# A macaron block: the written order of the first feed-forward's first two tiles

## The chip, the core and the metric

One core of one Trainium2 chip runs the whole kernel. The metric is the device time of one execution in microseconds (us), the median of several runs. The engines are TensorE (PE, with its weight loads PEld), VectorE (DVE), ScalarE (ACT), GpSimd (POOL) and SyncE (SP, which here only issues transfers). Each works through its own queue in order; they wait for each other by semaphores.

## What is computed

2048 tokens with 1024 features, all in float32, pass a feed-forward, an attention over a convolution, and the same feed-forward again:

```
x = x + 0.5 * ffn(layernorm(x))
x = x + attn(layernorm(x))
x = x + 0.5 * ffn(layernorm(x))

def ffn(x):                                   # weight 1024x1024, 8 experts
    routing   = softmax(x @ gate_w.T)
    in_scale  = routing @ in_channel_scale
    out_scale = routing @ out_channel_scale
    return (x * in_scale) @ sign(weight).T * out_scale + bias
```

The change is in the first feed-forward alone, in how its first tiles are put in order.

## The kernel before, in words

The first feed-forward works on 16 tiles of 128 tokens. A tile goes through these stages, each a method of `Ffn`:

- `norm`: mean and variance by DVE (`normalize`, L155 to L161), the inverse root by POOL as a power (L162), and the normalized row `xn` by ACT with a shift from POOL (L169, L170) or by DVE alone (L166).
- `add_bias` (L192): a transfer issued by POOL adds the halved bias `hbias` onto the token row in SBUF, for the residual.
- `transpose` (L200, L201): eight 128x128 transposes by PE in two banks of PSUM, copied to `xnT`.
- `gate` (L208, L216): PE multiplies with the gate weights, ACT copies the result `lgs`.
- `route` (L221 to L232): PE folds the logits (`lg`), DVE takes the maximum (L223), ACT the exp (L226), DVE the reciprocal and the routing in a high and a low part (`rhl`).
- `turn` (L239, L241): PE transposes the routing (`rt`), DVE copies it (`rT`).
- `scale` (L251 to L265): PE multiplies `rT` with a table of channel scales, `tables` (`is`, eight matmuls); for each half of 512 features DVE multiplies `xnT` with it, a high part `y` is rounded (L264, ACT), and POOL subtracts for the low part (L265).
- `out_scale` (L274, L276): PE makes the output scale (`po`), ACT halves it into `os`.
- `main` (L287 to L297): for each half of 512 outputs 16 matmuls of 128x512, high and low part of eight chunks against the signs of the weights, `sw`; DVE multiplies with `os` and adds to the token row.

Two tiles' chains run ahead of the main products. The loop `run` puts the stages of the tiles t+1 to t+4 around the two halves of tile t. After a tile's main product come the second norm and its transposes for the attention part (`norm_x2`, `transpose_x2`, L408 to L419).

The loop's instructions are ordered by a scheduler, while those of `begin`, L621 to L690, stand under `tc.manual_schedule()`: each engine gets them in the order of the program text. `begin` loads the gate weights and a bias row by ACT's queue, two token rows, six of the eight weight chunks and a third token row by SP's, and four pieces of the tables by POOL's. It builds `tables` from them (L664, `table_terms`: L142, L143), normalizes and transposes tiles 0 and 1, spreads the bias over 128 partitions by matmuls with a column of halves (`hb`, L659) that DVE copies (L660), and then goes tile 0 and tile 1 through gate, route, turn and scale. The signs of the weight chunks (L633, ACT) stand in between. Tile 0's main product takes both halves together, with tile 2's transposes and tile 3's norm between its chunks 5 and 6; the loop starts with tile 1.

Two sets of banks matter: `tr` (two banks) holds transposes and input scales in turn, `mm` (two) the main products. A small bias for the attention part each (`conv_b` to `bo`, L699) is loaded by POOL behind `begin`.

Of the kernel before, what the change touches and what calls it, by code (L numbers as in the profile page):

```python
# [24 lines left out]
def kernel(  # L25
# [87 lines left out]
    halves = const.tile([1, P], F32, name="halves")  # L113
    nc.gpsimd.memset(halves, 0.5)
# [13 lines left out]
    def table_loads(tmp):  # L128

        raw = tmp[:, 0, 0:NB]  # L130
        for n, src in enumerate((ics, ocs)):
            for h in range(NH2):
                nc.gpsimd.dma_start(
                    out=raw[ts(2 * n + h, QC), :],
                    in_=src[:, ts(h, NB)].unsqueeze(0).broadcast_to([4, E, NB]),
                )
        return raw

    def table_terms(raw, upper):


        nc.vector.tensor_scalar(raw, raw, lower, None, ALU.mult)  # L142
        nc.vector.scalar_tensor_tensor(tables, upper.bitcast(F32), sides, raw, ALU.mult, ALU.add)  # L143
# [7 lines left out]
    def normalize(dst, src, name, pinned=False, on_vector=False):  # L151

        stats = small.tile([P, NH2, 6], F32, name=f"st_{name}", tag="stats")
        for h in range(NH2):
            ins = nc.vector.bn_stats(out=stats[:, h, :], in_=src[:, ts(h, NB)])  # L155
            if pinned:
                pin(ins)
        mv = small.tile([P, 2], F32, name=f"mv_{name}", tag="mv")
        nc.vector.bn_aggr(out=mv, in_=stats)
        rstd = small.tile([P, 1], F32, name=f"rs_{name}", tag="rstd")  # L160
        nc.vector.tensor_scalar(rstd, mv[:, 1:2], EPS, None, ALU.add)  # L161
        nc.gpsimd.tensor_tensor(rstd, rstd, nhalf, ALU.pow)  # L162
        if on_vector:
            for h in range(on_vector):
                cols = ts(h, D // on_vector)
                nc.vector.tensor_scalar(dst[:, cols], src[:, cols], mv[:, 0:1], rstd, ALU.subtract, ALU.mult)  # L166
            return
        shift = small.tile([P, 1], F32, name=f"sh_{name}", tag="shift")
        nc.gpsimd.tensor_scalar(shift, mv[:, 0:1], rstd, -1.0, ALU.mult, ALU.mult)  # L169
        nc.scalar.activation(dst, src, AF.Identity, bias=shift, scale=rstd)  # L170

    class Ffn:
# [6 lines left out]
        def __init__(self, name, sw, work, xnp, first, end, row, ahead, after, between, beside, kept=1, leave=None):  # L179
            self.kept, self.leave = kept, leave or (lambda t, h: None)  # L180
            self.name, self.sw, self.work, self.xnp, self.first, self.end = name, sw, work, xnp, first, end
            self.row, self.ahead, self.after, self.between, self.beside = row, ahead, after, between, beside
            self.xns, self.xnTs, self.lgps, self.routs, self.rTs, self.oscs, self.ys = ({} for _ in range(7))

        def norm(self, t, pinned=False, on_vector=False):
            for n in range(t, min(t + 2, self.end)):
                self.ahead(n)
            self.xns[t] = self.xnp.tile([P, D], F32, name=f"xn_{self.name}_{t}", tag="xn")
            normalize(self.xns[t], self.row(t), f"{self.name}_{t}", pinned, on_vector)
# [4 lines left out]
        def transpose(self, t, copy=nc.scalar.copy):  # L194
            xn = self.xns.pop(t)
            xnT = self.work.tile([P, DC, P], F32, name=f"xnT_{self.name}_{t}", tag="xnT", bufs=3)
            for h in range(DC // 4):
                tr = bank("tr", [P, 4, P], f"tr_{self.name}_{t}_{h}")
                for c in range(4):
                    nc.tensor.transpose(tr[:, c, :], xn[:, ts(4 * h + c, P)], ident)  # L200
                copy(xnT[:, 4 * h : 4 * h + 4, :], tr)  # L201
            self.xnTs[t] = xnT
# [16 lines left out]
        def route(self, t):  # L219
# [6 lines left out]
            nc.scalar.activation(rout, lg, AF.Exp, bias=nmax, accum_out=rsum)  # L226
            nc.vector.reciprocal(rsum, rsum)
# [16 lines left out]
        def scale(self, t, copy=nc.scalar.copy, out=False):  # L244
# [15 lines left out]
            for h, sc in enumerate(scs):  # L260
                y = xnT[:, 4 * h : 4 * h + 4, :]
                nc.vector.tensor_tensor(y, y, sc, ALU.mult)
                yh, yl = (yhl[:, n, 4 * h : 4 * h + 4, :] for n in range(2))
                copy(yh, y)  # L264
                nc.gpsimd.tensor_tensor(yl, y, yh.bitcast(F32), ALU.subtract)  # L265
# [13 lines left out]
        def main(self, t, *halves, between=None, at=DC - 2):  # L279
            y, osc, xrow = self.ys[t], self.oscs[t], self.row(t)  # L280
            pms = {h: bank("mm", [P, NB], f"pm_{self.name}_{t}_{h}") for h in halves}
            for c in range(DC):
                if between and c == at:
                    between()
                for h, pm in pms.items():
                    for n in range(2):
                        nc.tensor.matmul(  # L287
                            pm,
                            lhsT=y[:, n, c, :],
                            rhs=self.sw[:, c, ts(h, NB)],  # L290
                            start=(c == 0 and n == 0),
                            stop=(c == DC - 1 and n == 1),
                        )
            for h, pm in pms.items():
                o, xt = osc[:, ts(h, NB)], xrow[:, ts(h, NB)]
                nc.vector.tensor_tensor(pm, pm, o, ALU.mult)  # L296
                nc.vector.tensor_tensor(xt, xt, pm, ALU.add)  # L297
                self.leave(t, h)
            if NH2 - 1 in pms:
                del self.ys[t], self.oscs[t]  # L300
# [19 lines left out]
        def run(self):  # L320
# [3 lines left out]
            for t in range(self.first, self.end):  # L324
                self.on(self.gate, t + 2)
                if t + 1 in self.ys:
                    self.out_scale(t + 1)
                elif t + 1 < self.end:
                    self.scale(t + 1, out=True)
                route, turn = (lambda stage=stage: self.on(stage, t + 2) for stage in (self.route, self.turn))  # L330
                begun = t not in self.ys
                if begun:
                    route()
                else:
                    self.main(t, 0, between=route, at=DC // 2)
# [4 lines left out]
                if begun:  # L340
                    turn()
                else:
                    self.main(t, 1, between=turn, at=DC // 2)
# [46 lines left out]
    def norm_x2(t):  # L390
        xn = x2ns[t] = xnp.tile([P, D], F32, name=f"x2n_{t}", tag="xn")
# [3 lines left out]
        normalize(xn, x1.pop(t), f"x2_{t}", on_vector=2 * (t + 1 == NT))  # L395
# [225 lines left out]
    def begin(ffn, work):  # L621
# [5 lines left out]
        def load_raw(c):  # L627
            raws[c] = cwp.tile([P, D], F32, name=f"raw_{c}", tag="cw")
# [6 lines left out]
        tmp = work.tile([P, 2, D], F32, name="tables_raw", tag="y")  # L635
        upper = work.tile([P, 2, D], F32R, name="tables_upper", tag="y")[:, 0, 0:NB]

        rows = work.tile([P, D], F32, name="gate_rows", tag="osc")[0:DC, :]
        brow = work.tile([P, D], F32, name="bias_row", tag="osc")[0:1, :]
        nc.scalar.dma_start(out=rows, in_=gate_t.rearrange("(c p) e -> c (p e)", p=P))  # L640
        nc.scalar.dma_start(out=brow, in_=bias)
        load_x(0)
        load_x(1)
        for c in range(6):
            load_raw(c)
        load_x(2)
        raw = table_loads(tmp)
# [5 lines left out]
        ffn.norm(0)  # L653
        ffn.norm(1, on_vector=True)
        ffn.transpose(0)
        ffn.transpose(1, nc.vector.tensor_copy)
        for h in range(NH2):
            hb = bank("acc", [P, NB], f"hb_{h}")
            nc.tensor.matmul(hb, lhsT=halves, rhs=brow[:, ts(h, NB)], start=True, stop=True)  # L659
            nc.vector.tensor_copy(hbias[:, ts(h, NB)], hb)  # L660
        ffn.add_bias(0)
        ffn.add_bias(1)
        ffn.gate(0)
        nc.scalar.copy(upper, raw)  # L664
        ffn.route(0)
        table_terms(raw, upper)
        ffn.gate(1)
        sign(0)
        load_raw(6)
        ffn.turn(0)  # L670
        ffn.route(1)
        sign(1)
        load_raw(7)
        load_x(3)
        ffn.scale(0)
        ffn.turn(1)
        sign(2, 3)
        ffn.scale(1, nc.vector.tensor_copy)
        sign(4, 5)
        ffn.norm(2, on_vector=True)  # L680
        ffn.add_bias(2)
        sign(6)
        ffn.out_scale(0)
        sign(7)

        def third():
            ffn.transpose(2, nc.vector.tensor_copy)
            ffn.norm(3, on_vector=True)
            ffn.add_bias(3)

        ffn.main(0, 0, 1, between=third)

    with ExitStack() as ph:
# [4 lines left out]
        for dst, src in ((conv_b_sb, conv_b), (bq_sb, bq), (bk_sb, bk), (bv_sb, bv), (bo_sb, bo)):  # L698
            tc.keep_in_program_order(nc.gpsimd.dma_start(out=dst, in_=src))  # L699
        ffn.run()  # L700
# [275 lines left out]
    ffn.run()  # L976
# [55 lines left out]
```

## Time and profile before

| what | value |
|---|---|
| runs | 976.38, 977.24, 980.49 us; median 977.24 |
| the profiled execution | 980.25 us; its span in the trace 978.0 us |
| granted TensorE clock, mean | 0.999 |
| DVE, ACT, POOL busy | 67%, 42%, 26% of the span |
| tile 3's first main matmul to tile 4's, tile 4's to tile 5's | 10.81, 10.84 us |
| HBM read, written | 81.18 MB, 37.85 MB |
| signs of the weights on ACT, one of 128x1024 | 1.05 us |
| low part on POOL, one of 128x512 | 1.28 us |
| add on DVE, one of 128x512 | 0.69 us |

In the profile's lines of instructions in order of time, the columns are the start and the length in us of a merged group, the engine, the line of the kernel, the operation, output <- inputs, sizes and the number of instructions; in brackets stands how long the engine sat idle before it, and what released it. In the lines of waits they are the waiting engine and line, what it waited for, and the total, the count and the longest in us. A timeline's name has no tile number, so tiles are told apart by their order.

### The profile page before, as it was taken

To read this page: it belongs to the slowest core of one execution; us is meant where nothing else is said; L and a number is where in the kernel's file an instruction comes from. 1 tells how busy PE (TensorE), PEld (TensorE's weight loads), DVE (VectorE), ACT (ScalarE), POOL (GpSimd) and SP (SyncE) were. 2 spreads that over 40 slices of the span, in tenths; PEclk is the share of its full clock that TensorE was granted. 3 is DMA by queue.
4 is the path that set the end of the run, shared out by engine and by line. 5 is a ranking of instruction groups with operands and counts; after the bars stand their busy time and mean duration, and the time that the engine had idled before them with its cause. 6 is when DMAs were issued, how large, how long until landed. Compare 5 with 4: busy or idle time off the path is not lost.

```text
span 978.0 us, 13872 instructions
## 1 busy us (share of the span) xinstructions
PE 955.0 (98%) x5068; PEld 624.4 (64%) x5068; DVE 652.0 (67%) x1229; ACT 409.4 (42%) x1117; POOL 256.1 (26%) x327
## 2 busy tenths in 40 slices
PE   5999999999999999999999999999999999999998
PEld 3778888776666666655555455545554556778776
DVE  4879887789976556636656455645565655777764
ACT  3576675331111111125546244526461663444440
POOL 3654553320011011003303121212122312444341
PEclk9999999999999999999999999999999999999999
DMA  8866653598496775335030430044003226646331
GB/s 251 235 164 193 183 174 131 196 274 332 155 276 183 183 183 122 93 108 226 15 116 1 152 113 17 1 151 151 1 1 139 62 39 210 173 135 174 108 108 65
DMA packets 36820, 136.69 MB, mean 140 GB/s; under 512 B 4297, under 2 KB 5321, under 8 KB 34834
## 3 DMA queue, kind: packets, MB, share of 16 engines
q1 hardware_dynamic: 27472, 98.15, 27.9%
q0 software_dynamic: 8544, 29.64, 15.9%
q10 hardware_dynamic: 738, 8.02, 2.2%
q8 instruction: 40, 0.66, 0.3%
q14 instruction: 26, 0.21, 0.1%
HBM read 81.18 MB, written 37.85 MB: 122 GB/s over the span
## 4 chain that ended last, share of the span: by engine, by line
PE 45%; issue 26%; POOL 5%; DVE 1%; DMA 0%; ACT 0%; POOLq 0%; DVEq 0%
PE cv L521 22%; PE pm_f L287 13%; POOL xr L807 3%; PE pp L941 2%; POOL p L863 2%; PE acc L922 2%; PE tr_f L200 1%; PE pq L830 1%; PE lgp_f L208 1%; PE is_f L251 1%; PE ao L905 1%; PE pt L892 1%; PE sc L851 0%; DMA qkv<-y 0%; DVE y L618 0%
## 5 line engine op out<-in xcount | busy, mean ns | idle before, releaser
L287 PE MATMUL pm_f<-sw,y_f 128*128 128x512 f32 x1024 | 263.6, 405 | 0.2 <-DVE x L297 0.2
L287 PEld LDWEIGHTS pm_f<-sw,y_f 128*128 128x128 f32 x1024 | 184.7, 189 | 40.6 <-DVE x L297 0.4
L521 PE MATMUL cv<-v,u 128*128 128x342 f32 x576 | 166.0, 450 | 0.0
L521 PEld LDWEIGHTS cv<-v,u 128*128 128x128 f32 x576 | 109.0, 189 | 56.8
L863 POOL TENSOR_SCALAR_AFFINE_SELECT p<-p 128x512 f32<-128x512 f32 x64 | 39.9, 647 | 282.1 <-ACT p L861 282.1
L876 ACT ACTIVATE p<-p,anm 128x128 f32<-128x128 f32 x256 | 99.0, 389 | 16.8 <-DVE anm L873 16.8
L265 POOL TENSOR_TENSOR y_f<-xnT_f,y_f 128x512 fp32r<-128x512 f32 x64 | 81.1, 1281 | 59.8 <-ACT y_f L264 59.0
L538 ACT ACTIVATE m<-cv 128x342 f32<-128x342 f32 x42 | 19.2, 457 | 159.0 <-PE cv L521 154.8
L861 ACT COPY p<-sc 128x512 f32<-128x512 f32 x64 | 34.3, 589 | 111.4 <-PE sc L851 111.3
L873 DVE TENSOR_REDUCE anm<-p 128x4 f32<-128x512 f32 x64 | 40.9, 681 | 49.1 <-POOL p L863 49.1
L296 DVE TENSOR_TENSOR pm_f<-pm_f,os_f 128x512 f32<-128x512 f32 x64 | 44.4, 694 | 35.4 <-PE pm_f L287 35.1
L922 PE MATMUL acc<-oT,wo_sb 128*128 128x512 f32 x128 | 67.2, 616 | 0.4 <-DVE oT L914 0.4
L830 PE MATMUL pq<-qkv,wq_sb 128*128 128x512 f32 x128 | 61.0, 596 | 0.0
L830 PE MATMUL pq<-qkv,wk_sb 128*128 128x512 f32 x128 | 60.1, 592 | 0.0
L521 PE MATMUL cv<-v,g 128*128 128x342 f32 (+2 forms) x224 | 57.1, 415 | 0.9 <-DVE v L443 0.9
L941 PE MATMUL pp<-pw_sb,o2T 128*128 128x512 f32 x128 | 57.4, 599 | 0.4
L814 PE MATMUL pv<-wv_sb,qkv 128*128 128x512 f32 x128 | 56.1, 592 | 0.0
L509 DVE SCALAR_TENSOR_TENSOR u<-g,u 128x1024 f32<-128x1024 f32 x18 | 22.0, 1222 | 43.7 <-issue 30.1
L521 PEld LDWEIGHTS cv<-v,g 128*128 128x128 f32 x224 | 39.7, 190 | 17.6 <-DVE v L443 1.3
L201 ACT COPY xnT_f<-tr_f 128x512 f32<-128x512 f32 x60 | 32.6, 590 | 42.0 <-PE tr_f L200 42.0
L876 ACT ACTIVATION_READ_ACCUMULATOR p<-p,anm 128x1 f32 x256 | 48.0, 188 | 0.0
L884 DVE TENSOR_TENSOR p<-p,asum 128x512 f32<-128x512 f32 x64 | 45.6, 712 | 2.4 <-DVE asum L883 0.3
(146 smaller groups left out, 1485.5 us busy)
## 6 DMA issues: line engine op xcount, KB each, us to landing
g<-in_conv_w_dram SPq DMA_DIRECT2D x28, 512.0 KB, 4.8
u<-in_conv_w_dram POOLq DMA_DIRECT2D x24, 512.0 KB, 6.3
x<-in_x_dram SPq DMA_DIRECT2D x16, 512.0 KB, 5.1
raw<-in_weight_t_dram SPq DMA_DIRECT2D x16, 512.0 KB, 7.0
x<-hbias POOLq DMA_DIRECT2D x16, 512.0 KB, 5.6
x<-x SPq DMA_DIRECT2D x16, 512.0 KB, 5.3
xr<-x SPq DMA_DIRECT2D x16, 512.0 KB, 7.1
x<-xr SPq DMA_DIRECT2D x16, 512.0 KB, 4.0
```

Of the source, the lines that this page charges most:

```text
L265: nc.gpsimd.tensor_tensor(yl, y, yh.bitcast(F32), ALU.subtract)
L287: nc.tensor.matmul(pm, lhsT=y[:, n, c, :], rhs=self.sw[:, c, ts(h, NB)], start=(c == 0 and n == 0), stop=(c == DC - 1 and n == 1),)
L296: nc.vector.tensor_tensor(pm, pm, o, ALU.mult)
L521: nc.tensor.matmul(accs[w, k][:, lo:hi], lhsT=uk[:, c, :], rhs=V[k][:, c, lo:hi], start=(c == 0), stop=(c == DC - 1),)
L814: nc.tensor.matmul(pv, lhsT=qkvs[g][2][:, c, ts(b, P)], rhs=wv_sb[:, c, ts(half, NB)], start=(c == 0), stop=(c == WC - 1),)
L830: nc.tensor.matmul(pq, lhsT=w_sb[:, c, ts(hp, P)], rhs=qkvs[g][n][:, c, :], start=(c == 0), stop=(c == WC - 1),)
L863: nc.gpsimd.affine_select(out=p, in_=p, pattern=[[0, BPG], [-1, P]], compare_op=ALU.is_ge, fill=NEG_INF, base=0, channel_multiplier=1,)
L873: nc.vector.tensor_reduce(nmax, p, AX.X, ALU.max, negate=True)
L876: nc.scalar.activation(p[:, b, :], p[:, b, :], AF.Exp, bias=nmax[:, b : b + 1], accum_out=asum[:, b : b + 1],)
L884: nc.vector.tensor_tensor(p, p, asum.unsqueeze(2).broadcast_to([P, BPG, P]), ALU.mult)
L922: nc.tensor.matmul(accs[g][m], lhsT=wo_sb[:, hp, ts(m, P)], rhs=oT, start=(hp == 0), stop=(hp == NHP - 1),)
L941: nc.tensor.matmul(pp, lhsT=o2T[:, m, ts(b, P)], rhs=pw_sb[:, m, ts(h, NB)], start=(m == 0), stop=(m == WC - 1),)
```

## The change

`begin` is written anew and goes further, to the end of tile 1's main product; the loop starts with tile 2.

- Loads: all eight weight chunks, the bias (spread over 128 partitions by the transfer itself), and token rows 2 to 5 are issued by SP at once. Weight chunks 6 and 7 lie in buffers of the token rows. The five small biases for the attention part go to SP's queue.
- The bias is halved by ACT in place. The column of halves, the four instructions of `hb` and their copies are gone.
- Norm is split into its sums and its application; tiles 0 to 3 are applied by DVE, tile 0 in two halves.
- Tile 0 goes through gate and route ahead of tile 1's transposes. The tables are made in two parts of 64 rows, the input scales' first, with DVE's product placed between the exp and the reciprocal.
- The low part of tile 0's first half is made by DVE.
- The stages of tiles 1 to 4 and signs 3 to 7 are put between the chunks of the main products of tiles 0 and 1. Tile 0's last two chunks are done for one half and then the other, and each half's end on DVE follows its last chunk.

```diff
+    def upper_terms(raw, upper, n):
+        nc.scalar.copy(upper[ts(n, P // 2), :], raw[ts(n, P // 2), :])
+
+    def lower_terms(raw, n):
+        at = ts(n, P // 2)
+        nc.vector.tensor_scalar(raw[at, :], raw[at, :], lower[at, :], None, ALU.mult)
...
-        def main(self, t, *halves, between=None, at=DC - 2):
...
+        def main(self, t, *halves, beside={}, apart=DC):
...
+            for c, h in [(c, h) for c in range(apart) for h in halves] + [
+                (c, h) for h in halves for c in range(apart, DC)
+            ]:
+                if h == halves[0] and c in beside:
+                    beside[c]()
...
+                if c == DC - 1:
+                    o, xt = self.oscs[t][:, ts(h, NB)], xrow[:, ts(h, NB)]
+                    nc.vector.tensor_tensor(pms[h], pms[h], o, ALU.mult)
+                    nc.vector.tensor_tensor(xt, xt, pms[h], ALU.add)
...
-        for h in range(NH2):
-            hb = bank("acc", [P, NB], f"hb_{h}")
-            nc.tensor.matmul(hb, lhsT=halves, rhs=brow[:, ts(h, NB)], start=True, stop=True)
-            nc.vector.tensor_copy(hbias[:, ts(h, NB)], hb)
...
+        for c in range(DC):
             load_raw(c)
+            if c == 5:
+                load_x(2)
+        nc.sync.dma_start(out=hbias, in_=bias.broadcast_to([P, D]))
+        load_x(3)
+        load_x(4)
+        load_x(5)
+        table_loads(raw)
...
+        on_vector = (nc.vector.tensor_copy,) * 2
+        ffn.norm_sums(0, on_vector=2)()
+        norm = ffn.norm_sums(1, on_vector=1)
+        ffn.transpose(0)
+        norm()
+        ffn.gate(0)
+        upper_terms(raw, upper, 0)
+        ffn.route(0, lambda: lower_terms(raw, 0))
+        table_terms(raw, upper, 0)
+        ffn.transpose(1)
+        ffn.turn(0)
+        sign(0, 1)
+        ffn.scale(0, lows=(nc.vector, nc.gpsimd))
+        upper_terms(raw, upper, 1)
+        lower_terms(raw, 1)
+        table_terms(raw, upper, 1)
+        ffn.gate(1)
+        sign(2)
...
+        def halve():
+            nc.scalar.mul(hbias, hbias, 0.5)
+
+        def sums(t, on_vector=False):
+            norms[t] = ffn.norm_sums(t, on_vector=on_vector)
+
+        def apply(t):
+            norms.pop(t)()
+
+        beside = {
+            1: part((sign, 3), (ffn.route, 1), (sums, 2, 1)),
+            2: part((sign, 4), (apply, 2)),
+            3: part((ffn.turn, 1), (sign, 5)),
+            4: part((sign, 6), (ffn.scale, 1), (sign, 7), (halve,), (ffn.add_bias, 1)),
+            5: part((ffn.transpose, 2, on_vector), (sums, 3, 1)),
+            6: part((ffn.out_scale, 0), (ffn.gate, 2)),
+        }
+        ffn.main(0, 0, 1, beside=beside, apart=DC - 2)
+        ffn.add_bias(0)
+        apply(3)
+        ffn.out_scale(1)
         ffn.add_bias(2)
...
+        ffn.main(1, 0, beside={
+            2: part((ffn.route, 2), (sums, 4)),
+            4: part((ffn.transpose, 3), (apply, 4), (ffn.add_bias, 4)),
+            6: part((ffn.turn, 2)),
+        })
+        ffn.gate(3)
+        ffn.scale(2, out=True)
+        ffn.add_bias(3)
+        ffn.main(1, 1, beside={
+            3: part((ffn.route, 3), (ffn.transpose, 4)),
+            5: part((ffn.turn, 3)),
+            6: lambda: (rest.append(x2_sums(0)), sums(5)),
+        })
+        ffn.gate(4)
+        rest[0]()
+        apply(5)
+        ffn.add_bias(5)
...
-            tc.keep_in_program_order(nc.gpsimd.dma_start(out=dst, in_=src))
-        ffn.run()
+            tc.keep_in_program_order(nc.sync.dma_start(out=dst, in_=src))
+        ffn.run(2)
```

## The prediction, made before the changed kernel ran

> **What bounds the kernel now.** I read the busy table and the 40 slices first, then TensorE's waits, then the first 75 us engine by engine in order of time. All times are us from the span's start.
>
> From the page:
>
> ```profile
> PE 955.0 (98%) x5068; PEld 624.4 (64%) x5068; DVE 652.0 (67%) x1229; ACT 409.4 (42%) x1117; POOL 256.1 (26%) x327
> ...
> PE   5999999999999999999999999999999999999998
> ```
>
> TensorE (PE) is busy 98% of the span; only the first slice (0 to 24.5) is a 5. So the change, which rewrites that start, can win only there. PE's waits say the same:
>
> ```profile
> PE tr_f L200 <- ACT xn_f L170: 5.2, 2, 4.7
> PE gt L651 <- DMA gate_rows<-in_gate_t_dram: 2.8, 1, 2.8
> PE is_f L251 <- DVE rT_f L241: 2.6, 4, 0.9
> ```
>
> PE's timeline shows how the start is spent (start, length, work, idle before):
>
> ```profile
> 8.53 3.76 PE L200 MATMUL tr_f<-ident,xn_f 128*128 128x128 f32 x16 [4.72 <-ACT xn_f L170]
> 12.22 3.77 PE L659 MATMUL hb<-bias_row,halves 1*128 1x512 f32 x4
> ...
> 24.56 6.88 PE L287 MATMUL pm_f<-sw,y_f 128*128 128x512 f32 x24
> ...
> 37.72 2.34 PE L287 MATMUL pm_f<-sw,y_f 128*128 128x512 f32 x9 [0.17 <-DVE x L297]
> ...
> 50.03 2.11 PE L287 MATMUL pm_f<-sw,y_f 128*128 128x512 f32 x8
> ```
>
> Main products, the real work, begin at 24.56 for tile 0, 37.72 for tile 1, 50.03 for tile 2. From tile 3 on the pace is steady; PE's later timeline has
>
> ```profile
> 63.17 2.11 PE L287 MATMUL pm_f<-sw,y_f 128*128 128x512 f32 x8
> ...
> 73.98 2.12 PE L287 MATMUL pm_f<-sw,y_f 128*128 128x512 f32 x8
> ```
>
> as the starts of tiles 3 and 4, and tile 5 starts at 84.82: 10.83 a tile, without a gap. In the built order of the changed kernel every engine has its old order again after tile 3, so the whole effect is how much earlier tile 4's product starts than 73.98. Behind it PE stays the bound (its waits list holds only single microseconds), so I take that lead to last to the end.
>
> ACT and DVE set the start. Two lines of ACT's timeline:
>
> ```profile
> 23.81 4.85 ACT L633 ACTIVATE sw<-raw 128x1024 fp32r<-128x1024 f32 x5
> 28.57 1.05 ACT L276 ACTIVATE os_f<-po_f 128x512 f32<-128x512 f32 x2
> ```
>
> a sign is 1.05 (its start-to-start 0.97), an output scale 0.53 a half.
>
> **Part by part, the new start.** I carry the new written order forward: each instruction starts when its engine is free and its input there, with the duration of its row before.
>
> *Gate and tables (to 14.2).* x_0 lands at 4.37, as before. Statistics 1.29, aggregate 0.21 and add 0.15 on DVE, the power on POOL 0.57: 6.82. The row is now applied by DVE in halves (0.81 for a whole row; a half near the 0.48 of the 128x512 table product) instead of by ACT (1.24), so PE starts transposing at 7.4, not 8.53. The half copies come 1.15 and 2.01 behind the first transpose (9.68 and 10.54 against 8.53): done at 9.1 and 10.0. Gate, its copy (0.27) and lg: the maximum starts at 11.6, against 18.02. The four matmuls hb (3.77) and two DVE copies of 0.69 are gone. From the maximum to the routing's last product took 1.36 (18.02 to 19.38); a half table product (0.48) fits in the wait for ACT's exp: 13.1. The other table product (0.75) ends at 13.85, tile 1's transposes at 13.3; turn (0.5) and copy (0.28): 14.2. A 64-row table operation may cost half or all of a 128-row one; I take all, since rows lie on separate partitions; halves would save at most 0.4.
>
> *First scale and first product (to 19.7).* Eight input-scale matmuls 1.1: 15.35; a product on DVE 0.67. ACT has signs 0 and 1 first (to 16.15), then the cast 0.61: 16.8. The low part of half 0 is now on DVE: no such row exists; the nearest are 0.69 (DVE x add) and 1.28 (POOL's low); I take 0.69: 17.5. So the main product starts at 17 instead of 24.56, 7 us earlier. But DVE is a queue: the second half's product stands behind that low part (18.15), its cast on ACT 18.8, the second table's copy 0.62 (19.4), and only then tile 1's gate copy, 19.7.
>
> *Where the lead goes.* PE holds tile 1's route behind four matmuls, and all other main matmuls queue behind it. lg_1 after 19.7; maximum at 20.6 (DVE is in the second table until then); exp behind sign 3 on ACT (22.1); routing 22.9. Behind it on DVE stand tile 2's statistics (1.62), the wait for POOL's power (0.57) and the row (0.81) *ahead of* tile 1's turn copy: 26.4. PE finishes chunk 3 by about 24.3 and waits some 2 us. Then scale 0.6, two products (28.4), casts (29.05), sign 7 (30.1), and the new halving of the bias: ACT's scaling of 128x1024 takes 1.05 (u, L502): 31.15, with the out-scale behind it, half 0 at 31.7. Four DVE operations of 0.69 (34.5), tile 3's row (35.3), tile 2's routing (36.7). Main product 0 ends at about 32.5 (34.1 before) and tile 1's begins at 32.8, against 37.72: still 5 us ahead.
>
> Tile 4's statistics 1.6 (38.3), power and shift on POOL (39.3), its row on ACT 1.24 (40.5), and on ACT behind it tile 3's gate copy, out-scale 1.05, casts 1.13, exp 0.35: 43.3. Tile 3's routing 44.05, for which PE waits 1.2. Six matmuls at 0.24 and then gate and scales 1.17 (72.81 to 73.98): tile 2's product starts at 46.8, against 50.03. Lead 3.2.
>
> *Tiles 2 and 3.* Before, tile 2 took 63.17-50.03 = 13.1, 2.3 more than steady. The same chain after 46.8: tile 0's second norm and tile 5's row on ACT end at 51.55 (0.6 of wait), its out-scale and cast delay exp_4 to 53.2, DVE's routing to 55.7 (0.5 of wait): tile 3 at 59.0. Lead 4.2. ACT is then behind: four copies of second-norm columns (1.6) and three rows of 1.24 stand ahead of tile 5's gate copy (61.85), which PE wants at 60.95: 0.95 lost. Tile 4 at 70.8: **lead 3.2**.
>
> *Transfers.* Five more loads of 512 KB follow the ninth (done at 16.2 by the rates second by second); at the 350 to 410 GB/s of that stretch each adds 1.3 to 1.4: raw 6 and 7, bias, x_3 to x_5 land at 17.6 to 24.6. Their readers come at 24.2, 29.05, 30.1, 30, 36.7 and 46: hidden, with 5 us or more to spare; without that cover each microsecond late would go one to one into ACT's chain. Row additions on POOL cost 0.9 each to issue, behind POOL's low parts; the first waits for the halving, which ends when POOL's work does (31.1). The five small biases leave POOL (0.87 each) for SP, ahead of x_6 and x_7, which wait for signs 6 and 7 anyway.
>
> [...] Sixteen transposes from 8.53 take 3.76 (0.235 each), later ones 0.10; main matmuls start 0.43 apart and run at 0.24 only from about 26.9. The clock column shows 1.00 throughout, so it does not show this pace. [...] In my sum slow matmuls before 26.4 cost nothing, as DVE is later than they.
>
> **The sum.** Against the profiled execution: 980.25 - 3.2 = 977.05 (its span is 978.0, 2.25 less). That execution lies 3.0 above the median shown, 977.24; against the median: 977.24 - 3.2 = **974.0**.
>
> **Rivals.** (a) *The waits in tiles 2 and 3 do not come*: the lead of 3.2 at tile 2's start meets steady tiles: 46.8 + 2 x 10.83 = 68.5, 5.5 ahead: 971.8. For: these waits hang on ACT's queue, where I count the latest of everything. Against: before, tile 2 had the same waits (2.3). (b) *The lead is gone by tile 4*: ACT runs later than I count, by 3 us: 977.2. For: before, DVE once sat idle for 3.4 waiting for tile 4's exp on ACT. (c) *PE's pace stays slow to the end of main product 0*: scale, twelve main matmuls, transposes and gate after 26.4 at twice the time: main product 0 ends near 38 instead of 32.5, tile 3's row 4.7 later: 978.7. For: broken PE work; against: before, 2.4 us of dense matmuls ended it. (d) *Slower: the broadcast bias lands late.* The halving stands on ACT ahead of both out-scales, tile 2's gate copy and its exp. From a landing at 30.1 each microsecond is paid; it decides from 33.3 (no lead left); at 40 it would give 977.24 + 6.7 = 984. For: one row read 128 times. Against: before, the same kind of load (projection bias) took 11.2 behind two others of 1 MB; so here I expect 20.
>
> **Chances.** Forecast 0.55 (972 to 976), (a) 0.25, (b) 0.10, (c) 0.05, (d) 0.05. About 0.5% (4.9 us) is what a measurement can tell from no change. Faster by that (under 972.4): (a) and the lower edge of the forecast, 0.34. Slower (over 982.1): (d) and a little of (c), 0.07. Within: 0.59. The range leaves out (d), half of what might lie beyond (a), and little else: 969.5 to 979.0. It takes in the unknown rows: the low part on DVE (up to 0.6 later), 64-row operations (0.4 earlier), pace at 26.4 (0.5 later).
>
> **What would show it.** First transposes at 7.4; first main matmul at 17; PE's waits for is_f after rT of tile 1 near 26.4 (2 us), for rt of tile 3 near 44 (1 us); tile 1's product at 33, tile 2's at 47, tile 3's at 59, tile 4's at 71; no DMA named as a releaser of ACT or DVE after 5. Wrong would be: the halving idle for its DMA, main matmuls 0.43 apart after 30, or a tile after the fourth that takes over 10.9.

## The result, and the profile after

The changed kernel takes 976.36 us (median of 19 runs, 975.42 to 977.77). The kernel before takes 978.77 us over the 19 runs that were made beside it and earlier (976.24 to 981.23), not 977.24 as in the three that the prediction had. The ratio is 0.9974, 95% interval 0.9966 to 0.9982: 2.4 us or 0.26% faster. That is less than the 0.5% that the prediction took for the least that can be told from no change, but the interval does tell it. The profiled execution took 976.54 us (its span is 974.4), 3.7 less than the profiled one of before, 980.25, which lies in the upper part of before's range.

The page of the changed kernel, busy time, TensorE's slices and its clock:

```profile
PE 952.4 (98%) x5064; PEld 622.2 (64%) x5064; DVE 653.8 (67%) x1228; ACT 411.7 (42%) x1122; POOL 251.7 (26%) x319
...
PE   6999999999999999999999999999999999999997
...
PEclk7999999999999999999999999999999999999999
```

TensorE is still the bound. Its first slice went from 5 to 6, and the clock row now shows a 7 there. The timeline of PE in the changed kernel (start, length, work, idle before it and what ended that):

```profile
7.28 1.97 PE L216 MATMUL tr_f<-ident,xn_f 128*128 128x128 f32 x8 [3.41 <-DVE xn_f L177]
...
15.82 2.37 PE L307 MATMUL pm_f<-sw,y_f 128*128 128x512 f32 x4 [0.39 <-ACT y_f L281]
...
25.11 0.66 PE L268 MATMUL is_f<-rT_f,tables 32*128 32x128 f32 x8 [0.33 <-DVE rT_f L258]
...
32.43 1.20 PE L307 MATMUL pm_f<-sw,y_f 128*128 128x512 f32 x4 [0.23 <-DVE x L320]
...
44.01 0.33 PE L256 MATMUL rt_f<-ident,rhl_f 128*128 128x128 f32 x1 [1.64 <-DVE rhl_f L249]
...
46.83 2.09 PE L307 MATMUL pm_f<-sw,y_f 128*128 128x512 f32 x8
...
58.11 2.12 PE L307 MATMUL pm_f<-sw,y_f 128*128 128x512 f32 x8
...
60.76 0.39 PE L237 MATMUL lg_f<-fold,lgs_f 128*128 128x8 f32 x2 [0.53 <-ACT lgs_f L232]
...
69.60 0.33 PE L268 MATMUL is_f<-rT_f,tables 32*128 32x128 f32 x2 [0.38 <-DVE rT_f L258]
...
70.24 2.11 PE L307 MATMUL pm_f<-sw,y_f 128*128 128x512 f32 x8
```

The first main product starts at 15.82 instead of 24.56: 8.7 us ahead. Against the rows of before, tile 1 is then 5.3 ahead (32.43), tile 2 3.2 (46.83), tile 3 5.1 (58.11), tile 4 3.7 (70.24), and tile 5 still 3.8 (81.06 against 84.82). So more than half of the early lead is given back by tile 4, and what is left there is what the two profiled executions differ by; the medians differ by 2.4. From tile 4's start to the end of the span it is 904.0 us before (978.0 - 73.98) and 904.2 after.

Tile 0's first four main matmuls take 2.37, twice what they take at full pace (1.20 at 32.43); the prediction had such slow matmuls up to 26.4. What it did not have is in the wait at 44.01: that ends with DVE's last product of the routing, L249, which takes 1.22. In a_route3, below, the same instruction takes 0.28. DVE and then POOL in the changed kernel:

```profile
42.73 1.22 DVE L249 SCALAR_TENSOR_TENSOR rhl_f<-ro_f,rsum_f,rhl_f 128x64 fp32r<-128x64 f32 x1
...
63.54 2.57 DVE L249 SCALAR_TENSOR_TENSOR rhl_f<-ro_f,rsum_f,rhl_f 128x64 fp32r<-128x64 f32 x1
```

```profile
41.37 2.50 POOL L282 TENSOR_TENSOR y_f<-xnT_f,y_f 128x512 fp32r<-128x512 f32 x2 [0.53 <-ACT y_f L281]
```

POOL's two low parts end at 43.87, DVE's small product at 43.95. The product of a later tile, at 63.54, takes 2.57.

### The profile page after: what moved, and what is told of

Its sections match the earlier page's. It is cut to its first block, busy times and chain, and to the rows that moved or that the text cites. A ratio compares the mean times of both kernels' runs of the same rounds, so it can differ in the third digit from the quotient of the medians.

```text
span 974.4 us, 13860 instructions
## 1 busy us (share of the span) xinstructions
PE 952.4 (98%) x5064; PEld 622.2 (64%) x5064; DVE 653.8 (67%) x1228; ACT 411.7 (42%) x1122; POOL 251.7 (26%) x319
## 4 chain that ended last, share of the span: by engine, by line
PE 60%; issue 28%; POOL 6%; DVE 4%; ACT 2%; DMA 1%; POOLq 0%; DVEq 0%; ACTq 0%
PE pm_f L307 23%; PE cv L539 22%; POOL xr L856 3%; PE tr_f L216 3%; PE pp L990 2%; POOL p L912 2%; PE lgp_f L224 2%; PE acc L971 2%; PE is_f L268 2%; PE tr L426 1%; PE pq L879 1%; PE ao L954 1%; PE pt L941 1%; PE po_f L291 0%; PE sc L900 0%
## 5 line engine op out<-in xcount | busy, mean ns | idle before, releaser
L307 PE MATMUL pm_f<-sw,y_f 128*128 128x512 f32 x1024 | 267.2, 408 | 0.6 <-ACT y_f L281 0.4
```

The source lines that it names most:

```text
L307: ins = nc.tensor.matmul(pms[h], lhsT=y[:, n, c, :], rhs=self.sw[:, c, ts(h, NB)], start=(c == 0 and n == 0), stop=(c == DC - 1 and n == 1),)
```

## The experiments

Three questions: which part of the change gives the 2.4 us; where the other 5 us of lead go; and what the half pace of TensorE costs. Each kernel was timed in five rounds beside the kernel before. Of each I give the median, the ratio to before with its 95% interval, and the start of tile 4's main product in its profile (before 73.98, changed kernel 70.24), which shows the lead that is left when the loop runs steadily. Such a start comes from one execution, in which TensorE's clock took a course of its own (see the last section).

**b_nohb: the kernel before, with the bias part alone.** The row additions of tiles 0 and 1, which need the bias, move behind its halving.

```diff
-        nc.scalar.dma_start(out=brow, in_=bias)
         load_x(2)
+        nc.sync.dma_start(out=hbias, in_=bias.broadcast_to([P, D]))
...
-        for h in range(NH2):
-            hb = bank("acc", [P, NB], f"hb_{h}")
-            nc.tensor.matmul(hb, lhsT=halves, rhs=brow[:, ts(h, NB)], start=True, stop=True)
-            nc.vector.tensor_copy(hbias[:, ts(h, NB)], hb)
...
         sign(4, 5)
+        nc.scalar.mul(hbias, hbias, 0.5)
```

> The kernel before with one part of the change alone: the bias comes by one spread transfer and is halved by ScalarE behind sign 5, and the four hb matmuls with their two copies are gone. Theory A (the start is one chain, and hb stands on it): tile 0's gate begins near 12.3 instead of 15.9, everything behind it some 3.5 us earlier, tile 4's main product near 70.5 instead of 74.0; 3 to 3.5 us faster than before, which is the whole gain of the change or more. Theory B (the new order earns the gain; hb is hidden, the routing chain waits elsewhere anyway): within 0.7 us of before.

Measured: 976.26 us, 0.9967 [0.9954, 0.9979], tile 4 at 70.67. PE's timeline of b_nohb:

```profile
11.87 0.64 PE L206 MATMUL lgp_f<-xnT_f,gate_sb 128*32 128x128 f32 x16
...
19.87 8.20 PE L285 MATMUL pm_f<-sw,y_f 128*128 128x512 f32 x24
...
34.34 2.35 PE L285 MATMUL pm_f<-sw,y_f 128*128 128x512 f32 x9 [0.18 <-DVE x L295]
...
70.67 2.12 PE L285 MATMUL pm_f<-sw,y_f 128*128 128x512 f32 x8
```

Tile 0's gate starts at 11.87 instead of 15.92, and of these 4.05 us 3.3 are still there at tile 4. This one part, with the old order, gives as much as the whole change: the intervals of the two ratios share 0.9966 to 0.9979.

**a_hb: the changed kernel, with the old bias part put back.** The four matmuls `hb` and their copies stand behind tile 1's transposes; the spread transfer and the halving by ACT are gone.

```diff
         ffn.transpose(1)
+        for h in range(NH2):
+            hb = bank("acc", [P, NB], f"hb_{h}")
+            nc.tensor.matmul(hb, lhsT=halves, rhs=brow[:, ts(h, NB)], start=True, stop=True)
+            nc.vector.tensor_copy(hbias[:, ts(h, NB)], hb)
         ffn.turn(0)
...
-        nc.sync.dma_start(out=hbias, in_=bias.broadcast_to([P, D]))
```

> The changed kernel with one part undone: the bias again by four hb matmuls and two VectorE copies, placed behind tile 1's transposes, no spread transfer and no halving. Theory A (hb stands on the chain in either order): hb takes 2.0 at full clock or 3.8 at half, its copies stand ahead of tile 0's turn copy, so tile 0's scale comes 1.4 to 3.2 later and so does all behind it: 1.4 to 3.2 us slower than the changed kernel. Theory B (the new order hides hb, so both parts are needed together): within 0.5 of it.

Measured: 981.80 us, 1.0026 [1.0012, 1.0039], tile 4 at 75.32: slower than before, and 5.1 later at tile 4 than the changed kernel, more than expected. PE's timeline of a_hb:

```profile
13.53 3.78 PE L690 MATMUL hb<-bias_row,halves 1*128 1x512 f32 x4
17.23 0.47 PE L258 MATMUL rt_f<-ident,rhl_f 128*128 128x128 f32 x1
18.38 1.11 PE L270 MATMUL is_f<-rT_f,tables 32*128 32x128 f32 x8 [0.67 <-DVE rT_f L260]
...
20.89 2.38 PE L309 MATMUL pm_f<-sw,y_f 128*128 128x512 f32 x4 [0.38 <-ACT y_f L283]
...
75.32 2.11 PE L309 MATMUL pm_f<-sw,y_f 128*128 128x512 f32 x8
```

The routing of tile 0 was ready at 13.2 and waited until 17.23 behind the four matmuls; the first main product is 5.1 later (20.89), and nothing gives that back. With the row of before it makes a table of tile 4's start:

| order of the start | bias by matmuls | bias by one transfer |
|---|---|---|
| old | 73.98 | 70.67 |
| new | 75.32 | 70.24 |

The bias part is worth 3.3 in the old order and 5.1 in the new; the rest of the rewrite is worth 0.4 with it and loses 1.3 without. The ratios of the times give the bias part 3.2 us in the old order and 5.1 in the new. By them the rest is worth nothing that can be told with the transfer (0.9974 against 0.9967) and loses some 2.5 us without it (1.0026).

**a_route3: tile 3's gate copy and route ahead of tile 4's row and tile 2's scale**, so that the routing doesn't run while POOL makes the low parts.

```diff
-            4: part((ffn.transpose, 3), (apply, 4), (ffn.add_bias, 4)),
+            4: part((ffn.transpose, 3)),
...
         ffn.gate(3)
-        ffn.scale(2, out=True)
-        ffn.add_bias(3)
+        apply(4)
+        ffn.add_bias(4)
         ffn.main(1, 1, beside={
-            3: part((ffn.route, 3), (ffn.transpose, 4)),
+            1: part((ffn.route, 3)),
+            2: lambda: (ffn.scale(2, out=True), ffn.add_bias(3)),
+            4: part((ffn.transpose, 4)),
```

> The changed kernel with tile 3's gate copy and route ahead of tile 4's row and of tile 2's scale on every engine. Theory A (TensorE's wait of 1.6 for tile 3's routing comes from ScalarE's queue, where the exp stood behind the out-scale and the casts, and from the routing's last product on VectorE, 1.22 instead of 0.28 while GpSimd made low parts): that wait goes and the product takes 0.28: 1.3 to 1.6 us faster than the changed kernel, tile 2's product at 45.3. Rival: tile 2's low parts come later by as much and its main product waits for them: no change (within 0.4).

Measured: 975.11 us, 0.9956 [0.9944, 0.9969], tile 2 at 45.95 and tile 4 at 69.37: the wait at 44 is gone, 1.25 us gained on the changed kernel's median, a little less than expected. Its five runs (974.90 to 975.37) all lie below the lowest of the changed kernel (975.42). DVE's timeline of a_route3:

```profile
40.70 0.28 DVE L249 SCALAR_TENSOR_TENSOR rhl_f<-ro_f,rsum_f,rhl_f 128x64 fp32r<-128x64 f32 x1
```

POOL's low parts run from 42.33 in it. The edit moved both the place in ACT's and DVE's queues and the overlap with POOL; of the 1.64 of wait, the 0.94 by which L249 is shorter is the share that goes with the overlap.

**a_turn1: tile 1's turn copy ahead of tile 2's row on DVE.** The prediction's wait of 2 us before tile 1's input scales was only 0.33 in the profile. Is this copy still what the start waits for?

```diff
-            2: part((sign, 4), (apply, 2)),
-            3: part((ffn.turn, 1), (sign, 5)),
+            2: part((sign, 4)),
+            3: part((ffn.turn, 1), (apply, 2), (sign, 5)),
```

> The changed kernel with tile 1's turn copy ahead of tile 2's row on VectorE. Theory A as predicted (the copy behind statistics, power and row holds TensorE 2 us): 1.5 to 2 us faster. Theory C after the trace (at half clock TensorE ends chunk 3 at 24.78, only 0.33 before the scale starts, so the slow pace has eaten that wait): 0.2 to 0.4 faster, not to be told from the changed kernel by its time; in the trace tile 1's scale follows chunk 3 without a wait.

Measured: 976.97 us, 0.9971 [0.9960, 0.9983], tile 4 at 71.01. No gain: the copy ends at 24.54 and PE goes from chunk 3 to the input scales without a wait (25.74), but its main matmuls before them run at half pace (eight in 3.76 at 20.13), so the copy was early for nothing. That tile 4 is 0.8 later than in the changed kernel is no measure of the edit: in this execution tile 1's transposes run at half pace (1.95 instead of 1.07), and tile 0's product, which stands ahead of the edit, starts at 16.77 instead of 15.82.

**a_lowpool: tile 0's first low part back on POOL.**

```diff
-        ffn.scale(0, lows=(nc.vector, nc.gpsimd))
+        ffn.scale(0)
```

> The changed kernel with tile 0's first low part on GpSimd again. The low part is done at 17.1 instead of 16.5, but VectorE's second product stands no longer behind it: its cast ends 1.3 earlier, the second table's copy and tile 1's gate copy with it (17.3 instead of 18.7). Theory A (tile 1's routing is the chain): routing 0.7 to 1.2 earlier and 0.3 to 0.7 us faster than the changed kernel. Rival (GpSimd's low parts hold VectorE's second table, as they seem to hold the routing's last product): nothing gained, 0 to 0.3 slower.

Measured: 976.32 us, 0.9973 [0.9964, 0.9983], tile 4 at 69.51: the median is that of the changed kernel. PE waits 0.55 for POOL's first low part, and 1.13 for tile 1's turn copy, which here comes 0.8 earlier, as the second half's product doesn't stand behind a low part on DVE. The 0.7 by which tile 4 is earlier in this profile is not in the median.

**a_all: these three edits together.** 

> The changed kernel with three edits together: tile 3's route early, tile 1's turn copy ahead of tile 2's row, both low parts of tile 0 on GpSimd. If each is worth what its own theory says and they add: 1.25 (measured for the first) plus 0.3 plus 0.3 to 0.7, so 1.8 to 2.3 us faster than the changed kernel (974.1 to 974.6). If half clock bounds TensorE up to 25, the last two add nothing: as the first alone, near 975.1.

Measured: 974.63 us, 0.9958 [0.9944, 0.9972], tile 4 at 68.71. It is 1.7 below the changed kernel, and its interval covers that of a_route3 alone: what the two other edits add isn't shown.

**b_warm and a_warm: eleven dense matmuls on zeros ahead of the first transposes**, to bring TensorE to full pace sooner, in the kernel before and in the changed one.

```diff
+        nc.vector.memset(warm.bitcast(F32), 0.0)
+        heat = bank("mm", [P, NB], "heat")
...
+                nc.tensor.matmul(heat, lhsT=warm[:, 0:P], rhs=warm, start=True, stop=True)
...
+        dense(3)
         gt = bank("sm", [P, E, DC], "gt")
...
+        dense(8)
```

> The kernel before with eleven added dense matmuls of 128x512 on zeros into a spare bank, three ahead of the gate weights' transposes and eight behind them (0.7 to 7.3 us, where TensorE stands idle); the output is unchanged. Theory C (TensorE's slow pace of the first 27 us is what both starts pay): granted clock full from about 5, transposes of tiles 0 and 1 in 1.6 instead of 3.8, hb in 1.9 instead of 3.8, tile 0's product at full pace: 3 us faster or more, and a smaller spread. Theory A (other engines set most of the chain; the slow pace comes back at the first gaps): 0 to 1.5 us faster.

> The changed kernel with the same eleven dense matmuls. In its trace the granted clock is 0.5 from 14.3 to 24.5, and chunks 0 to 3 of tile 0's product run at half pace there. Theory C: clock full to 25, chunks 0 to 3 in half the time; but tile 1's turn copy ends at 25.05 on VectorE's queue, so at most the 1.0 of tile 0's transposes and 0.5 of gate are saved: 1 to 1.5 us faster than the changed kernel. Theory A: the clock falls back at the gaps behind 9 anyway: 0 to 0.7 faster than the changed kernel.

Measured: b_warm 976.96 us, 0.9980 [0.9968, 0.9992], tile 4 at 72.08; a_warm 977.52, 0.9981 [0.9972, 0.9990], tile 4 at 71.49. The memset ran late, the dense matmuls lasted to 9.45 and 9.60, and the first transposes came at 9.29 and 9.40 instead of 8.53 and 7.28. In a_warm the pace was half again from 16.6 on all the same (four main matmuls in 2.37 at 17.00, the clock column at 0.50 from 17 to 23); it doesn't tell what the half pace costs the changed kernel, as the first transposes came 2.1 later and the half pace was still there. b_warm does tell something of the kernel before. PE's timeline of b_warm:

```profile
11.64 1.98 PE L669 MATMUL hb<-bias_row,halves 1*128 1x512 f32 x4
```

The matmuls `hb` take 1.98 at full pace instead of 3.77, tile 0's product starts 2.9 earlier (21.62) although the transposes came later, and 1.9 of that is left at tile 4. So part of what `hb` costs in the kernel before is the half pace at which it runs.

**a_fill and all_fill: the same idea with the right sizes**, in the changed kernel and in a_all.

```diff
+        nc.vector.memset(warm.bitcast(F32), 0.0)
         small_constants()
+        dense(4)
...
+        dense(6)
...
         ffn.gate(0)
+        dense(1)
...
         ffn.transpose(1)
+        dense(2)
         ffn.turn(0)
+        dense(2)
...
         sign(2)
+        dense(1)
...
-            1: part((sign, 3), (ffn.route, 1), (sums, 2, 1)),
+            1: part((sign, 3), (dense, 4), (ffn.route, 1), (sums, 2, 1)),
```

> The changed kernel with small dense matmuls on a block of zeros in TensorE's gaps from 1.5 to 19 us, which keep it busy and write to a bank that nothing reads: four ahead of the gate weights' transposes, six behind, then one, two, two, one and four more. Meant to bring TensorE to its full pace before the first main product without pushing the first transposes (7.28). If they do, 128x512 matmuls start 0.24 apart, not 0.46, from 16 us on. Theory C (the slow pace only fills time that TensorE would wait for tile 1's turn copy): is_f of tile 1 then waits 1 to 3 us for rT, and tile 4's product starts at 69.5 to 70.3, time 975.6 to 976.4, beside 70.24 and 976.36. Rival D (the slow pace itself sets the start): tile 4's product at 67 to 68.5, time 973 to 974.5.

> The same added matmuls in the kernel with all three edits (tile 3's route ahead, tile 1's turn copy ahead of tile 2's row, tile 0's low part on GpSimd). Here the copy that TensorE would wait for is early. Rival D: the freed TensorE time is a gain, tile 1's input scales at 21 to 23 instead of 24.63, tile 4's product at 66.7 to 68, time 972.6 to 974.0, beside 68.71 and 974.63. Theory C widened (ScalarE's signs, one per 0.97 us, are the next bound): TensorE waits for ACT (sw or y) in tile 0's chunks 4 to 7, tile 4's product within 0.4 of 68.7, time within 0.5 of 974.6.

PE's timeline of a_fill:

```profile
15.78 0.50 PE L307 MATMUL pm_f<-sw,y_f 128*128 128x512 f32 x1 [0.39 <-ACT y_f L281]
...
18.94 2.10 PE L307 MATMUL pm_f<-sw,y_f 128*128 128x512 f32 x8
...
25.08 0.66 PE L268 MATMUL is_f<-rT_f,tables 32*128 32x128 f32 x8 [1.98 <-DVE rT_f L258]
...
32.40 1.19 PE L307 MATMUL pm_f<-sw,y_f 128*128 128x512 f32 x4 [0.24 <-DVE x L320]
...
103.37 0.33 PE L268 MATMUL is_f<-rT_f,tables 32*128 32x128 f32 x2 [1.17 <-DVE rT_f L258]
```

This is the run that settles the pace. Eight main matmuls take 2.10 instead of 3.76 in the changed kernel, TensorE is at full pace from 16 us on, and it then waits 1.98 for tile 1's turn copy: input scales at 25.08 (25.11), tile 1 at 32.40 (32.43), tile 4 at 70.23 (70.24). In the changed kernel the half pace only filled a wait. The time of a_fill is nevertheless higher than that of the changed kernel, 978.01 us, 0.9988 [0.9978, 0.9998]: in its profile a wait of 1.17 at 103.37, deep in the loop, where a token row landed 1.8 later. In all_fill the same row is late too: DVE waits 3.02 for it and TensorE 0.63. In the changed kernel, before, b_nohb, a_route3 and a_all DVE waits 1.4 to 1.8 for it and TensorE not at all. Why the row is late with the added matmuls stays open.

all_fill: 974.07 us, 0.9944 [0.9927, 0.9962], tile 4 at 68.35, the lowest median of all; beside a_all's 974.63 the intervals overlap. Here four of the added matmuls ran at half pace (1.91 at 18.50, beside 1.09 at 17.30 in a_fill) and held TensorE to 20.2, ahead of tile 1's logits: it doesn't tell what full pace would be worth with all waits removed. From 20.2 to tile 1's product TensorE is idle for only 0.6.

## Why the prediction was right

**The sum.** Forecast: a lead of 3.2 at tile 4, and so 974.0. Measured: 3.74 at tile 4, 3.6 in the span, 2.4 between the medians. The absolute time was missed mostly because three runs of before were a low sample: 978.77 - 3.2 = 975.6, 0.8 below what was measured. That a lead at tile 4 lasts to the end holds to about 1.5 us only: from tile 4's start to the end of the span the profiled executions of the twelve kernels take 902.6 (b_warm) to 905.6 (a_fill). Of a change of 2.4 us, a single profile can't show the last microsecond.

**The carried order.** First transposes 7.4, measured 7.28; first main product 17, measured 15.82 (ACT's signs 0 and 1, booked to 16.15, were done at 14.9); tile 1 32.8 and 32.43; tile 2 46.8 and 46.83; tile 3 59.0 and 58.11; tile 4 70.8 and 70.24. The three prices without a row were taken rightly: the low part on DVE took 0.69, a 64-row table product 0.48 like a 128-row one (the second took 0.96, beside POOL's low part), the halving 1.04 without a wait for its transfer. The "five more loads" are six, as the prediction's own list and landing times have them.

**The wait for tile 1's turn copy** was forecast with TensorE through chunk 3 at 24.3 and the copy done at 26.4, some 2 us. Measured: 24.78 and 25.05, and a wait of 0.33. The copy came 1.35 earlier than carried, as tile 1's logits were folded at 18.72 and not after 19.7, and chunk 3 ended 0.5 later, as all its matmuls ran at half pace (four in 1.99 at 22.79, beside 1.21 at 25.70). That "slow matmuls before 26.4 cost nothing, as DVE is later than they" was right, and a_fill shows it: at full pace the wait is 1.98, and nothing behind it moves.

**The wait at 44** was put down to ACT's queue (exp at 43.3, routing 44.05, 1.2 of wait). Its place and size came out, 44.01 and 1.64, but by two errors that cancel, and that is luck. ACT's exp was done at 42.1, 1.2 earlier than booked. DVE's three small operations behind it took 1.9 instead of 0.75, as the last took 1.22 instead of 0.28 beside POOL's low parts. With 0.75 the wait would have been about 0.5, an estimate from these rows.

**Which part pays.** The prediction booked the removed `hb` inside one chain with the new order, and traced the lead to the order's earlier stages. The runs part the two: the removed `hb` alone is worth 3.3 at tile 4, the order 0.4. At the first main product the new order is 4.0 ahead of b_nohb (15.82 and 19.87). By tile 1 half of that is gone (32.43 and 34.34), behind DVE's copy at 25; by tile 2 all of it (46.83 and 46.66), with the wait of 1.64 at 44.

**Rivals.** (a), no waits in tiles 2 and 3, came by half: 0.2 in tile 2 where 1.1 was forecast, but 0.53 and 0.38 in tile 3 beside the forecast 0.95. The 0.38 is not for ACT, as forecast, but for a copy on DVE, whose queue L249 had held for 2.57. Tile 2 so took 11.28 (forecast 12.2), tile 3 12.13 (11.8), and the time is not that of this rival. (b) and (d) did not come: no DMA ends a wait of ACT or DVE between 5 and 100, and the one at 100.07 (1.83, a token row) is in before too (1.65 at 103.71). (c) did not come in the changed kernel, whose pace is full from 24.6 (four main matmuls in 1.21 at 25.70).

**The clock.** The prediction carried slow matmuls up to 26.4. In the changed kernel the pace became full near 11 (eight transposes in 1.97 at 7.28, in 1.07 at 11.21) and half again at 14.3, with no gap over 0.62 in between. Stretches of the changed kernel, each a third of the 10.24 us that the half pace lasts in it (bounds, length, PE busy with its count, granted clock, DMA share, GB/s):

```profile
10.91:14.32 3.41, 2.18 (x19) 1.00 1.02 401
14.32:17.73 3.41, 3.02 (x22) 0.50 1.02 408
17.73:21.15 3.42, 2.89 (x9) 0.50 1.02 405
21.15:24.56 3.41, 3.41 (x10) 0.50 0.86 301
```

Before the fall TensorE was busy 2.18 of 3.41 us; it rose again behind a stretch that was busy throughout. The busy share alone doesn't decide it: the rise at 10.91 came behind 3.42 us of which 3.00 were busy, while 3.02 busy from 14.32 to 17.73 did not bring the pace back, and in a_warm it stays full behind 23.41 to 26.82 with 2.02 busy. In before 7.4 us of unbroken work from 8.53 to 15.9 left the pace slow (sixteen gate matmuls in 1.08 at 17.91, beside 0.64 at 34.07), and main matmuls, 0.43 apart from 24.56, were 0.24 apart from about 26.9. What decides stays open. The half pace cost nothing here only because DVE was later (a_fill, at full pace, waits 1.98 for it).

## What to carry to other kernels

Before a start is rewritten as a whole, take the one thing out of the chain that stands in it for nothing (here four matmuls and two copies that spread a bias which is needed only where the first products end) and time that alone: here it gave as much as the whole rewrite. A lead at the first product is not a gain until it is still there when the loop is steady; read the start of the same stage some tiles later. And when two stages move beside each other, look at which engines then work at the same time (here DVE's product took 1.22 instead of 0.28 beside POOL's low parts), not only at the queues.

## What the hardware showed that was not expected

**DVE and POOL.** A DVE product of 128x64 takes 0.28, and in three places where POOL makes low parts 1.22 to 2.57, ending 0.08 behind POOL each time: 59.03 against 58.95 (before), 43.95 against 43.87 and 66.11 against 66.03 (after). A DVE product of 64x512 (L140) takes 0.96 at 18.41, instead of 0.48, beside the low part that POOL makes from 17.82 to 19.09. A DVE product of 128x512 that reads PSUM keeps its 0.69 inside POOL's low parts (before, L262 at 24.66; POOL from 23.39 to 25.91). The 2.57 from 63.54 last through both of POOL's low parts (63.51 to 66.03), the 1.22 from 42.73 lie beside the second alone (42.62 to 43.87).

**The steps of the clock.** By the clock column, its two edges worked out from the means of stretches of 1 us, the half pace lasts 10.24 us in the changed kernel, in a_route3, b_nohb and b_warm, 6.84 in a_lowpool and a_warm, 3.42 in all_fill: three, two and one times 3.41. So two profiles of kernels that differ by one edit can differ by 3.4 us or more of slow matmuls. From the column alone the first stretch can't be read: it shows 1.00 from the start on, while eight transposes take 1.97 at 7.28 and 1.07 at 11.21.

**The clock and the spread of the times.** The length of the half stretch is no fixed property of a kernel: its executions differ in it. Of the 62 runs of before that were timed beside the experiments, the 11 with a mean granted clock of 0.994 or 0.995 have a median of 977.29 us, the 15 with 0.992 or 0.993 have 978.63, the 28 with 0.999 or 1.000 have 979.72, and the 8 with 0.997 or 0.998 have 981.73. Of the 19 runs of the changed kernel the four with 0.994 or 0.995 have 975.79, the 15 with 0.999 or 1.000 have 976.37. A mean near 1.000 doesn't stand for full pace at the start, as the profile of before (0.999) shows with its main matmuls 0.43 apart up to 26.9. So the changed kernel is faster by 1.5 us in the first of these pairs and by 3.4 in the other, and the two profiles that this document compares, 0.999 and 0.994, are not of one pair.
